# Two spectral layers and a scan on one core: row transforms moved into the items, the projections and the scan's output

## The chip, the cores and the metric

The kernel runs on one core of one Trainium2 chip. The metric is the time of one execution in device microseconds (us). The kernel before took 3879.38 us (median of 3 runs, 3878.82 to 3880.02).

## The reference

An image of 48 x 48 positions and 768 channels, in 32-bit floats, goes through four layers: a vision transformer block, a spectral layer, a scan and a second spectral layer with other weights. The change touches the last three. Cut to what matters (a pair of numbers in `w[0], w[1]` is real and imaginary part):

```python
def spectral(x):                          # layers 1 and 3
    xs = rfft2(x, axes=(1, 2)).reshape(B, H, W // 2 + 1, 8, 96)
    xr, xi = real(xs), imag(xs)
    o1r = relu(xr @ w1[0] - xi @ w1[1] + b1[0])   # per block of 96 channels
    o1i = relu(xi @ w1[0] + xr @ w1[1] + b1[1])
    o2r = o1r @ w2[0] - o1i @ w2[1] + b2[0]
    o2i = o1i @ w2[0] + o1r @ w2[1] + b2[1]
    out = softshrink(o2r, 0.01) + 1j * softshrink(o2i, 0.01)
    return irfft2(out, s=(H, W), axes=(1, 2)) + x

def scan(x):                              # layer 2
    B_, C_, X, alpha, theta, gamma = projections(x)   # x @ W + b, silu or sigmoid
    for i in range(12):
        inj = rope(B_, theta * (i + 1)) * X
        h = alpha * conv3x3_depthwise(h) + (1 - gamma) * alpha * prev + gamma * inj
        prev = inj
    return silu((rope(C_, theta * 12) * h).reshape(48, 48, 256) @ W_out + b_out)
```

## The kernel before

**Names.** TensorE is PE, VectorE DVE, ScalarE ACT, GpSimd POOL and SyncE SP; SP only issues DMAs. The 768 channels are cut into two halves of 384 (`TB`), each into three column tiles of 128 (`ct`) and four blocks of 96 (`b`). The 48 image rows are cut into 6 groups `g` of 8 rows. `yu[half]` is a scratch array in DRAM that holds the half-spectrum along w of one half of the channels. A matmul of 32-bit floats is two instructions in the profile.

**The instructions' order.** Each engine carries out its instructions in an order that is fixed when the kernel is built. The program text sets it roughly; the builder moves instructions that are ready ahead of others, and loads above all. Waits come from the tiles: a tile of a pool with `bufs` buffers is free again when the last reader of its predecessor is done.

**First spectral layer, `afno_first` (L1529).** The transform along w (`spectrum_rows` L1361, here within `afno_follow`) is largely carried out in the layer before. `spectrum_mix` then works on 40 items: half (1, then 0), five groups of frequencies `kc`, four blocks `b`. An item is pipelined over 5 steps by a table of stages: the transform along h (`f_x`, L1420), first matrix (`f_o`, L1434 to L1436), second matrix and softshrink (`f_z`, L1455 to L1461) and the transform back along h (`f_u`, L1470). There are 44 steps; the last four, in which no new item begins, are the drain. After four blocks the tile `us` is stored to `yu` on SP (L1477). When all items are done, the transform back along w follows for half 1, then half 0: for each g the tile `gt` is loaded on SP (`load_spectrum` L1491, three buffers), and for each of 3 column tiles four matmuls with `gt` as the stationary operand and `iw` as the moving one (L1557) fill a PSUM bank, which ACT or DVE in turn copies into `x2T`, the scan's input with the channels on the partitions: 6 column tiles of 48 rows of 64 columns.

**Scan, `scan_phase` (L1000).** It opens with the DVE's memset of four pairs of PSUM banks `pss` (L1043) and POOL's memsets of the state (`H`, `al`, `c1`, `s0`, `s1`: L1045 to L1047). Then come the projections: for each of 24 pairs of image rows `pr`, two groups of 6 matmuls (357 and 256 columns, L1082) into one pair of banks, which DVE empties, adding the bias (L1084). After each 3 pairs a chain of DVE and ACT instructions makes sines, sigmoids and products of them (8 blocks `q`). The scan's 12 steps follow. Its output (L1230 to L1246): for each two pairs of rows (`p2`, 12 of them) four transposes, a copy on ACT to `hT`, then for each pair and half two matmuls (L1243), the bias on DVE (L1245) and silu on ACT (L1246) into `x3`.

**Second spectral layer, `afno_second` (L1564).** After the scan's output: the transform along w for 12 groups (half 0, then 1, L1361; stored on SP), `spectrum_mix` with half 0 first, and the transform back for half 0, then half 1: load `gt` (four buffers), four matmuls (L1588), the addition into `x3` on DVE (L1590), and the store to the output on ACT's queue (L1594), or, for the last group of each half, four stores on ACT's and SP's queues in turn (L1592).

Of the kernel before, what the change touches and what calls it, by code (L numbers as in the profile page):

```python
# [11 lines left out]
F32 = mybir.dt.float32  # L12
BF16 = mybir.dt.bfloat16
AF = mybir.ActivationFunctionType
ALU = mybir.AluOpType
AX = mybir.AxisListType
PSUM = bass.MemoryType.PSUM
DRAM = bass.MemoryType.DRAM

P = 128  # L20
# [979 lines left out]
def scan_phase(tc, ident, w, w_close, wts, xT, xT_close, c_d, cr_d, out_open):  # L1000
# [21 lines left out]
    with tc.tile_pool(name="sc_s", bufs=1, side="left") as sp:  # L1022
# [9 lines left out]
        with (  # L1032
# [9 lines left out]
            for ps in pss:  # L1042
                V.memset(ps, 0.0)  # L1043
# [4 lines left out]
            with (  # L1048
# [10 lines left out]
                def temp(shape, tag, q, bufs=1):  # L1059
                    return tp.tile([P, *shape], F32, tag=tag, name=f"{tag}_{q}", bufs=bufs)[:K]  # L1060
# [10 lines left out]

                for q in range(NQ):
# [3 lines left out]
                    for t in range(R4):  # L1076
                        tok = (q * R4 + t) * P
                        ps = pss[(q * R4 + t) % 4]
                        parts = ((za, 0, NA), (g, NA, NCR))
                        for i, (z, c0, n) in enumerate(parts):  # L1080
                            for cc in range(NC):
                                nc.tensor.matmul(ps[:K, i, :n], lhsT=xT[:, cc, tok : tok + K], rhs=w[:, cc, c0 : c0 + n], start=cc == 0, stop=cc == NC - 1)  # L1082
                        for i, (z, c0, n) in enumerate(parts):
                            V.tensor_tensor(z[:, :, t], ps[:K, i, :n], bias[:K, c0 : c0 + n], ALU.add)  # L1084
# [30 lines left out]
                    gc = temp([NM, R4], "gc", q)  # L1115
# [27 lines left out]
            w_close()  # L1143
            xT_close()
# [80 lines left out]
        with (  # L1225
            tc.tile_pool(name="so_t", bufs=3, side="left") as tp,
            tc.tile_pool(name="so_q", bufs=2, space=PSUM) as pt,
            tc.tile_pool(name="so_p", bufs=6, space=PSUM) as pm,
        ):
            for p2 in range(NPR // 2):  # L1230
                ps = pt.tile([P, 512], F32, tag="t", name=f"ht_{p2}")
                for t in range(2):
                    for j in range(2):
                        nc.tensor.transpose(ps[:, (2 * t + j) * P : (2 * t + j) * P + K], hg[:K, 2 * p2 + t, j * P : (j + 1) * P], ident[:K, :K])
                hT = tp.tile([P, 4, 2, G], F32, tag="hT", name=f"hT_{p2}")
                nc.scalar.copy(hT, ps.rearrange("p (i s w) -> p i s w", i=4, s=2)[:, :, :, :G])
                for t in range(2):
                    pr = 2 * p2 + t
                    for half in range(2):
                        cols = slice(half * TB, (half + 1) * TB)  # L1240
                        ps = pm.tile([P, 512], F32, tag="m", name=f"so_{pr}_{half}")
                        for j in range(2):
                            nc.tensor.matmul(ps[:BS, :TB], lhsT=hT[:, 2 * t + j].rearrange("p s w -> p (s w)"), rhs=wo[:, j, cols], start=j == 0, stop=j == 1)  # L1243
                        t_ = tp.tile([BS, TB], F32, tag="t", name=f"st_{pr}_{half}")
                        V.tensor_tensor(t_, ps[:BS, :TB], bo[:, cols], ALU.add)  # L1245
                        nc.scalar.activation(x3[:, pr, cols], t_, AF.Silu)  # L1246
    return x3
# [15 lines left out]
def block_kernel(ctx: ExitStack, tc: tile.TileContext, a: dict):  # L1263
# [69 lines left out]
    x2T, x2T_close = opened("x2T", [P, NC, G * HD], "right")  # L1333
    wsc, wsc_close = opened("wsc", [P, NC, a["W_scan"].shape[1]], "right")
    afno_first(tc, a, yu, x2T, follow_in, lambda: nc.sync.dma_start(wsc, a["W_scan"].rearrange("(c p) n -> p c n", p=P)))
# [11 lines left out]
    x3 = scan_phase(tc, ident, wsc, wsc_close, wts, x2T, x2T_close, c_d, cr_d, out_open)  # L1347
    afno_second(tc, a, x3, yu)
# [17 lines left out]
def spectrum_mix(tc, name, a, layer, yu, psum, keep, side, halves, beside):  # L1366
# [8 lines left out]
    w1, b1, w2, b2 = (a[f"{layer}_{k}"] for k in ("w1", "b1", "w2", "b2"))  # L1375
    HB = NB // 2
    with (
        tc.tile_pool(name=f"{name}_c", bufs=1, side=side) as cp,
        tc.tile_pool(name=f"{name}_y", bufs=3, side=side) as yp,
        tc.tile_pool(name=f"{name}_s", bufs=2, side=side) as sp,  # L1380
    ):
        fh = cp.tile([BS, BS], F32, tag="fh", name=f"{name}_fh")
        nc.sync.dma_start(fh, a["fh"])
        w1t = cp.tile([BS, NB, 2, BS], F32, tag="w1", name=f"{name}_w1")
        w1s, w1d = (cp.tile([BS, NB, BS], F32, tag=n, name=f"{name}_{n}") for n in ("w1s", "w1d"))
        w2t = cp.tile([BS + 1, NB, 2, BS], F32, tag="w2", name=f"{name}_w2")
        b1t = cp.tile([BS, 2, NB], F32, tag="b1", name=f"{name}_b1")
        ih = cp.tile([BS, BS], F32, tag="ih", name=f"{name}_ih")
        ys = {}

        def load(half, kc):
            yt = yp.tile([BS, KC, TB], F32, tag="yt", name=f"{name}_yt_{half}_{kc}")
            nc.sync.dma_start(yt, yu[half][4 * KC * kc : 4 * KC * (kc + 1)].rearrange("(k q) p c -> (q p) k c", q=4))
            us = sp.tile([BS, KC, TB], F32, tag="us", name=f"{name}_us_{half}_{kc}")
            ys[half, kc] = yt, us

        nc.sync.dma_start(w1t, w1)
        nc.sync.dma_start(b1t, b1)
        nc.sync.dma_start(w2t[:BS], w2)
        nc.sync.dma_start(w2t[BS : BS + 1], b2)  # L1400
        nc.sync.dma_start(ih, a["ih"])
        nc.gpsimd.tensor_tensor(w1s, w1t[:, :, 0, :], w1t[:, :, 1, :], ALU.add)
        nc.gpsimd.tensor_tensor(w1d, w1t[:, :, 1, :], w1t[:, :, 0, :], ALU.subtract)
# [9 lines left out]
        def s_fft_h(i):  # L1413
            half, kc, b = items[i]
            if b == 0:
                load(half, kc)
# [112 lines left out]
def afno_first(tc, a, yu, x2T, follow_in, load_next):  # L1529

    nc = tc.nc
    ev = Evac(nc)
    x2v = x2T.rearrange("p c (h w) -> p c h w", w=HD)
    nc.gpsimd.memset(x2v[:, :, :, G:], 0.0)
    with (
        tc.tile_pool(name="f1_g", bufs=1, side="right") as gp,  # L1540
        tc.tile_pool(name="f1_p", bufs=8, space=PSUM) as pm,
    ):

        def psum(tag):
            return pm.tile([P, 512], F32, tag="m", name=f"f1_{tag}")

        iw = gp.tile([4 * KW, BS], F32, tag="iw", name="f1_iw")
        follow = follow_in(gp, 1)
        spectrum_mix(tc, "f1", a, "L1", yu, psum, True, "left", (1, 0), lambda step: follow(psum) if step in (1, 4) else load_next() if step == 8 else None)
        nc.sync.dma_start(iw, a["iw"])  # L1550
        for half in (1, 0):
            for g in range(NTB):
                gt = load_spectrum(nc, gp, yu, half, g, "f1", 3)
                for ct in range(NC // 2):
                    ps = psum(f"w_{half}_{g}_{ct}")
                    for i in range(4):
                        nc.tensor.matmul(ps[:, i * BS : (i + 1) * BS], lhsT=gt[: 4 * KW, i, ct * P : (ct + 1) * P], rhs=iw, start=True, stop=True)  # L1557
                    ev(x2v[:, half * NC // 2 + ct, 8 * g : 8 * g + 8, :G], ps[:, :TB].rearrange("p (h w) -> p h w", w=G))


def afno_second(tc, a, x3, yu):
# [4 lines left out]
    with (  # L1566
        tc.tile_pool(name="f3_g", bufs=1, side="left") as gp,
        tc.tile_pool(name="f3_p", bufs=8, space=PSUM) as pm,
    ):
# [3 lines left out]
        nc.sync.dma_start(iw, a["iw"])  # L1573

# [3 lines left out]
        for half in range(2):  # L1578
            for g in range(NTB):
                spectrum_rows(nc, fw, x3[:, 4 * g : 4 * g + 4, half * TB : (half + 1) * TB], yu, half, g, psum, gp, ev, "f3")  # L1580
        spectrum_mix(tc, "f3", a, "L3", yu, psum, False, "left", (0, 1), lambda step: None)
        for half in range(2):
            cols = slice(half * TB, (half + 1) * TB)
            for g in range(NTB):
                gt = load_spectrum(nc, gp, yu, half, g, "f3", 4)
                for i in range(4):
                    ps = psum(f"w_{half}_{g}_{i}")
                    nc.tensor.matmul(ps[:BS, :TB], lhsT=iw, rhs=gt[: 4 * KW, i, :], start=True, stop=True)  # L1588
                    dst = x3[:, 4 * g + i, cols]
                    nc.vector.tensor_tensor(dst, ps[:BS, :TB], dst, ALU.add)  # L1590
                    if g == NTB - 1:
                        (nc.scalar, nc.sync)[i % 2].dma_start(out[:, 4 * g + i, cols], dst)  # L1592
                if g < NTB - 1:
                    nc.scalar.dma_start(out[:, 4 * g : 4 * g + 4, cols], x3[:, 4 * g : 4 * g + 4, cols])  # L1594
# [112 lines left out]
```

## Time and profile before

| | before |
|---|---|
| median of 3 runs | 3879.38 us |
| the profiled execution | 3878.45 us |
| its span in the profile | 3876.6 us |
| PE busy | 3761.5 us, 97% of the span |
| DVE, ACT, POOL busy | 2059.0, 1141.9, 658.4 us |
| DMA | 460.43 MB, 119 GB/s |
| first layer's items end, transform back along w begins | 3049.3 us |
| projections | 3112.5 to 3264.1 us |
| first matmul of the scan's steps | 3275.6 us |
| scan's output and transform along w | 3528.5 to 3630.8 us |
| second layer's items | 3634.5 to 3830.8 us |
| last DVE addition | 3873.4 us |

The span is the time between the first and the last instruction of the profiled execution; 1.85 us lie around it. All points in time in the text are counted from the span's start. A line of groups shows engine and operation, output and inputs with their shapes, the number of instructions, then busy time, mean ns of one, and the idle time ahead of them with what ended it. A line of the timeline shows start, duration, instruction, and in brackets the wait ahead of it. The clock is the share of TensorE's full clock that was granted.

### The profile page before, as it was taken

The numbers are of one execution on the slowest core, as the hardware profiler recorded it, in microseconds if no ns is written. First come the engines' busy times: TensorE is split into PE (matmuls) and PEld (weight loads), VectorE is DVE, ScalarE is ACT, GpSimd is POOL, SyncE is SP. The second block draws the span as 40 slices with busy tenths as digits, with TensorE's granted clock in tenths as the row PEclk, the third lists the DMA queues.
The fourth block names the chain that finished last, engine by engine and source line by source line (L and its number), as shares of the span: only waits on it lengthen the run. The fifth ranks groups of instructions, "written<-read, shape, count | busy, mean of one in ns | idle before, by whom it ended". The sixth has DMA issues, their size and how long they took to land. (4 is left out here: it accounts for less than half of the span.)

```text
span 3876.6 us, 54460 instructions
## 1 busy us (share of the span) xinstructions
PE 3761.5 (97%) x22018; PEld 2285.7 (59%) x22018; DVE 2059.0 (53%) x3185; ACT 1141.9 (29%) x1907; POOL 658.4 (17%) x496
## 2 busy tenths in 40 slices
PE   8999989999999999998999999999999998999998
PEld 4666544444444444455555555555568866996685
DVE  6655456666666666555425333232335367995355
ACT  1322244444444444421310120021023246223341
POOL 3101011111111111024000000000023301981131
PEclk9999989999999999999999999999999799999999
DMA  7656563424232322134334434433454302110444
GB/s 257 210 187 197 173 183 112 127 92 133 84 110 83 105 87 76 36 95 161 123 105 155 150 107 124 147 122 108 132 139 110 96 24 93 40 32 22 146 108 159
DMA packets 266810, 460.43 MB, mean 119 GB/s; under 512 B 32989, under 2 KB 219349, under 8 KB 260055
## 3 DMA queue, kind: packets, MB, share of 16 engines
q1 hardware_dynamic: 256919, 436.23, 36.3%
q10 hardware_dynamic: 9632, 20.65, 1.4%
q8 instruction: 175, 2.87, 0.3%
q14 instruction: 84, 0.69, 0.1%
HBM read 318.49 MB, written 138.31 MB: 118 GB/s over the span
## 5 line engine op out<-in xcount | busy, mean ns | idle before, releaser
L576 DVE TENSOR_TENSOR acc<-acc,p 128x768 f32<-128x768 f32 x576 | 582.8, 1012 | 354.9 <-ACT p L568 316.5
L568 ACT ACTIVATE p<-s 128x768 f32<-128x768 f32 x648 | 478.5, 812 | 692.7 <-PE s L566 580.5
L929 PE MATMUL p<-w,h 128*128 128x384 f32 x1512 | 492.7, 486 | 0.0
L558 PE MATMUL s<-qt,kv 64*128 64x384 f32 x2592 | 478.5, 501 | 9.1 <-ACT p L568 7.4
L587 PE MATMUL av<-p,kv 128*64 128x384 f32 x2592 | 464.5, 493 | 0.0
L929 PEld LDWEIGHTS p<-w,h 128*128 128x128 f32 x1512 | 286.1, 190 | 196.9
L558 PEld LDWEIGHTS s<-qt,kv 64*128 64x128 f32 x2592 | 233.1, 187 | 249.9 <-ACT p L568 116.0
L587 PEld LDWEIGHTS av<-p,kv 128*64 128x64 f32 x2592 | 170.0, 136 | 225.2 <-issue 215.8
L866 PE MATMUL p<-x2nT,w 128*128 128x384 f32 x864 | 294.0, 490 | 3.1 <-issue 3.1
L294 PE MATMUL qk<-xnT,wqk 128*128 128x384 f32 x756 | 252.5, 491 | 5.2 <-DMA wqk<-wqk_d 5.2
L1172 PE MATMUL c<-H,bands 128*48 128x96 f32 x5632 | 242.8, 247 | 12.1 <-issue 11.5
L566 PE MATMUL s<-bt,oneh 120*128 120x384 bf16 x1296 | 248.3, 328 | 0.0
L1172 PEld LDWEIGHTS c<-H,bands 128*48 128x48 f32 x5632 | 234.2, 123 | 20.9 <-issue 11.9
L866 PEld LDWEIGHTS p<-x2nT,w 128*128 128x128 f32 x864 | 165.4, 192 | 119.1 <-issue 6.0
L866 PE MATMUL p<-xT,w 128*128 128x384 f32 x648 | 220.8, 486 | 0.0
L566 PEld LDWEIGHTS <-oneh 120*128 120x128 bf16 x1296 | 109.1, 98 | 174.3 <-issue 115.1
L294 PEld LDWEIGHTS qk<-xnT,wqk 128*128 128x128 f32 x756 | 144.6, 193 | 99.9 <-issue 8.5
L905 POOL TENSOR_TENSOR rr<-rr,ml_b 128x1152 f32<-128x1152 f32 x12 | 33.5, 2788 | 954.4 <-DMA rr<-xr_d 660.8
L861 ACT ACTIVATE h<-h,ml_b 128x384 f32<-128x384 f32 x144 | 88.3, 614 | 346.6 <-DVE h L881 174.3
L1180 POOL TENSOR_TENSOR t<-s,c 128x768 f32<-128x768 f32 x80 | 144.8, 1836 | 214.3 <-DVE s L1142 203.8
L866 PEld LDWEIGHTS p<-xT,w 128*128 128x128 f32 x648 | 123.1, 190 | 85.9
L1082 PE MATMUL c<-wsc,x2T 128*112 128x357 f32 (+1 forms) x576 | 151.6, 426 | 2.0 <-DVE c L1043 2.0
(314 smaller groups left out, 4778.7 us busy)
## 6 DMA issues: line engine op xcount, KB each, us to landing
w<-w1s_d SPq DMA_DIRECT2D x36, 768.0 KB
w<-w2s_d SPq DMA_DIRECT2D x36, 768.0 KB
bt<-rh_d SPq DMA_DIRECT2D x144, 162.0 KB
w<-w1s_d SPq DMA_DIRECT2D x36, 576.0 KB
w<-in_mlp_w_dram SPq DMA_DIRECT2D x27, 768.0 KB
wqk<-wqk_d SPq DMA_DIRECT2D x12, 1344.0 KB
yu<-f_ys SPq DMA_DIRECT2D x24, 672.0 KB
f_gt<-yu SPq DMA_DIRECT2D x24, 672.0 KB
```

The lines of the kernel that those rows point to most:

```text
L294: nc.tensor.matmul(p[:, :TB], lhsT=w[:, n, c, :], rhs=ops[sb][n][:, c, :], start=c == 0, stop=c == NC2 - 1)
L558: nc.tensor.matmul(ps[:, s, :QB], lhsT=keys[pr % 2][rows, kt * P : (kt + 1) * P], rhs=qbs[qc % 2][0][rows], start=True, stop=False)
L566: nc.tensor.matmul(ps[:, s, :QB], lhsT=oneh[:NBR, b % 3, :], rhs=qbs[qc % 2][1][:NBR, s, b // 3, j, :], start=False, stop=True)
L568: nc.scalar.activation(p, ps[:, :, :QB], AF.Exp)
L576: nc.vector.tensor_tensor(probs[c], probs[c], p, ALU.add)
L587: nc.tensor.matmul(avs[c][rows, :QB], lhsT=vals[pr % 2][:, kt, rows], rhs=p[:, s, :], start=kt == 0, stop=kt == NT - 1)
L861: nc.scalar.activation(h, h, AF.Gelu, bias=b1c[:, k : k + 1])
L866: nc.tensor.matmul(p[:, :TB], lhsT=w[n][:, c, :], rhs=rhs[n][:, c, :], start=c == 0, stop=c == NC2 - 1)
L929: nc.tensor.matmul(ps[t][:, :TB], lhsT=hs[left, f][:, t * P : (t + 1) * P], rhs=wt[:, f % KW2, :], start=f == 0, stop=f == NF2 - 1)
L1082: nc.tensor.matmul(ps[:K, i, :n], lhsT=xT[:, cc, tok : tok + K], rhs=w[:, cc, c0 : c0 + n], start=cc == 0, stop=cc == NC - 1)
L1172: nc.tensor.matmul(ps[r0 : r0 + G, k // 4, cols], lhsT=bands[:, n - GC, i, :] if gr else bands0[:, n, i, :], rhs=H[:, n, :, d : d + NPR], ...
L1180: GP.tensor_tensor(t, sc[:, ch], c1[:, m0 : m0 + GC].unsqueeze(2).to_broadcast([P, GC, RR, NPR]), ALU.mult)
```

## The change

It has three parts.

1. *First spectral layer and projections.* `x2T` is replaced by `xh`, which holds half 1 only, and two small tiles `homes` of 8 image rows each for half 0. Half 1's transform back for g = 0 to 3 is issued within the drain (steps 40 to 43), with `gt` loaded at steps 28, 30, 32 and 34 (four buffers instead of three), and for g = 4 and 5 after it. Half 0's transform back of one group (`rows_back`) is called within the projections: ahead of the first pair of rows, and then at every fourth (`pr % 4 == 2`, for the group after the current one). Its column tiles use the two banks of the fourth PSUM pair in turn; the projections keep three pairs. The sum over the 6 column tiles runs in reverse, half 1 first. The temporary `gc` takes the buffer of `th`.
2. *Scan's output.* It becomes a generator with two passes: half 0 for all 12 `p2`, then half 1, with the 12 tiles `hT` kept. After every second `p2` the caller issues `spectrum_rows` of the group before, in the same pass, with the scan's PSUM banks. The second layer's weights (`spectrum_open`, split off from `spectrum_mix`) are loaded at the scan's end; the first three tiles of half 0's spectrum are loaded during the second pass.
3. *Second spectral layer.* Half 0's transform back is issued within the items, at steps 32, 35, 38, 40, 41 and 42, with its first four loads at steps 27, 29, 31 and 33. Only half 1's stays behind the items, with four loads ahead. The last group of half 0 is stored in one piece.

```diff
-            for ps in pss:
+            for ps in pss[:3]:
                 V.memset(ps, 0.0)
...
+                turn_of = itertools.cycle(range(2))
+                banks = lambda tag: pss[3][:, next(turn_of), :]
+                xs = [rows_back(0, banks)]
...
-                        tok = (q * R4 + t) * P
-                        ps = pss[(q * R4 + t) % 4]
+                        pr = q * R4 + t
+                        if pr % 4 == 2 and pr + 4 < NPR:
+                            xs.append(rows_back(pr // 4 + 1, banks))
+                        x_of = lambda cc: (xs[pr // 4], cc, pr % 4 * P) if cc < NC // 2 else (xh, cc - NC // 2, pr * P)
+                        ps = pss[pr % 3]
...
-                            for cc in range(NC):
-                                nc.tensor.matmul(ps[:K, i, :n], lhsT=xT[:, cc, tok : tok + K], rhs=w[:, cc, c0 : c0 + n], start=cc == 0, stop=cc == NC - 1)
+                            for cc in reversed(range(NC)):
+                                v, c, tok = x_of(cc)
+                                nc.tensor.matmul(ps[:K, i, :n], lhsT=v[:, c, tok : tok + K], rhs=w[:, cc, c0 : c0 + n], start=cc == NC - 1, stop=cc == 0)
...
-            for p2 in range(NPR // 2):
+            yield x3, psum
+            hTs = []
+            for half in range(2):
+                cols = slice(half * TB, (half + 1) * TB)
+                for p2 in range(NPR // 2):
+                    if half == 0:
...
+                        hT = tp.tile([P, 4, 2, G], F32, tag=f"hT{p2}", name=f"hT_{p2}", bufs=1)
...
+                    yield
...
+        def back(half, g, dst, psum):
+            gt = gts.pop((half, g))
+            for ct in range(HC):
+                ps = psum(f"w_{half}_{g}_{ct}")
+                for i in range(4):
+                    nc.tensor.matmul(ps[:, i * BS : (i + 1) * BS], lhsT=gt[: 4 * KW, i, ct * P : (ct + 1) * P], rhs=iw, start=True, stop=True)
+                ev(in_rows(dst)[:, ct, :, :G], ps[:, :TB].rearrange("p (h w) -> p h w", w=G))
...
+        def first_back(g):
+            back(1, g, xh[:, :, 8 * g * HD : 8 * (g + 1) * HD], psum)
+            if g + 4 < NTB:
+                load(1, g + 4)
...
+            elif last - 12 <= step < last - 4 and step % 2 == 0:
+                load(1, (step - last + 12) // 2)
+            elif step >= last:
+                first_back(step - last)
...
+        for g in range(4, NTB):
+            first_back(g)
+            load(0, g - 4)
...
+    def rows_back(g, banks):
+        if g + 2 < NTB:
+            load(0, g + 2)
+        back(0, g, homes[g % 2], banks)
+        return homes[g % 2]
...
+        def rows_in(n, psum):
+            half, g = ready[n]
+            spectrum_rows(nc, fw, x3[:, 4 * g : 4 * g + 4, half * TB : (half + 1) * TB], yu, half, g, psum, gp, ev, "f3")
+            if NTB <= n < NTB + 3:
+                opened[1](0, n - NTB)
...
+        for n, _ in enumerate(scan):
+            if n and n % 2 == 0:
+                rows_in(n // 2 - 1, scan_psum)
+            if n == 4 * NTB - 1:
+                rows_in(2 * NTB - 1, scan_psum)
...
-        for half in range(2):
-            for g in range(NTB):
-                spectrum_rows(nc, fw, x3[:, 4 * g : 4 * g + 4, half * TB : (half + 1) * TB], yu, half, g, psum, gp, ev, "f3")
-        spectrum_mix(tc, "f3", a, "L3", yu, psum, False, "left", (0, 1), lambda step: None)
...
+        loads = {items - 13 + 2 * g: g for g in range(4)}
+        backs = {items - 8: 0, items - 5: 1, items - 2: 2, items: 3, items + 1: 4, items + 2: 5}
+
+        def beside(step):
+            if step in loads:
+                load(0, loads[step])
+            if step in backs:
+                g = backs[step]
+                back(0, g)
+                if g + 4 < NTB:
+                    load(0, g + 4)
+
+        spectrum_mix(tc, "f3", opened, yu, psum, False, "left", (0, 1), beside)
+        for g in range(4):
+            load(1, g)
+        for g in range(NTB):
+            back(1, g)
+            if g + 4 < NTB:
+                load(1, g + 4)
```

## The prediction

> **What bounds the kernel now.** I read first the page, for the engine that bounds and for its clock.
>
> ```profile
> PE 3761.5 (97%) x22018; PEld 2285.7 (59%) x22018; DVE 2059.0 (53%) x3185; ACT 1141.9 (29%) x1907; POOL 658.4 (17%) x496
> ...
> PEclk9999989999999999999999999999999799999999
> ```
>
> PE is busy for 97% of the span, so waits can give back only 115 us in all. The clock is the second lever: the 32nd slice (96.9 us each, so 3004 to 3101) runs at 0.7. That is where the first spectral layer ends. So I asked for a table of stages around the three edits (us; then PE, PEld, DVE, ACT, POOL; clock; DMA share; GB/s).
>
> ```profile
> core 0: us, PE busy (x) PEld busy (x) DVE busy (x) ACT busy (x) POOL busy (x), PEclk, DMA share, GB/s
> 3049.00:3111.00 62.00, 61.46 (x290) 61.01 (x288) 10.63 (x19) 9.90 (x19) 23.19 (x6) 0.51 0.42 125
> 3112.00:3264.00 152.00, 151.53 (x576) 102.63 (x576) 111.06 (x282) 86.71 (x147) 0.00 (x0) 0.98 0.08 24
> 3264.00:3276.00 12.00, 0.49 (x7) 0.47 (x8) 9.96 (x32) 10.16 (x19) 0.00 (x0) 0.68 0.86 315
> 3528.00:3598.00 70.00, 68.71 (x235) 35.64 (x233) 28.02 (x52) 30.39 (x60) 0.00 (x0) 0.98 0.01 2
> 3598.00:3631.00 33.00, 31.85 (x97) 16.66 (x96) 11.76 (x23) 10.05 (x24) 3.58 (x2) 1.00 0.76 237
> 3631.00:3650.00 19.00, 12.66 (x57) 10.81 (x58) 2.79 (x7) 5.04 (x12) 3.64 (x5) 0.56 0.66 208
> 3650.00:3830.00 180.00, 177.02 (x1464) 148.56 (x1464) 89.92 (x175) 72.44 (x171) 54.93 (x75) 1.00 0.31 82
> 3830.00:3877.00 47.00, 36.74 (x98) 16.98 (x98) 27.24 (x49) 0.00 (x0) 0.00 (x0) 0.88 0.84 284
> ```
>
> Three rows are weak. The back-transforms of the first spectral layer (first row) fill PE at half clock. The start of the second layer's items (3631 to 3650) is a third idle and at half clock. The tail (last row) has the DMA engines at 84%. The projections (second row) are full of PE work at full clock, while DVE and ACT are busy for 111 and 87 of 152 us.
>
> Then the groups of the first row, and PE's timeline just before it:
>
> ```profile
> L1557 PE MATMUL f_w<-f_iw,f_gt 100*128 100x96 f32 x288 | 61.2, 419 | 0.0
> L1557 PEld LDWEIGHTS f_w<-f_iw,f_gt 100*128 100x128 f32 x288 | 61.1, 331 | 0.5 <-issue 0.5
> ```
>
> ```profile
> 3044.18 1.05 PE L1470 MATMUL f_u<-f_Z,f_ih 96*96 96x480 f32 x2 [1.43 <-DVE f_Z L1461]
> ...
> 3048.45 1.02 PE L1470 MATMUL f_u<-f_Z,f_ih 96*96 96x480 f32 x2 [1.53 <-DVE f_Z L1461]
> 3049.30 5.05 PE L1557 MATMUL f_w<-f_iw,f_gt 100*128 100x96 f32 x25
> ```
>
> 288 instructions in 61.2 us are 212 ns apart. The stage begins after a drain in which PE waited 1.43 and 1.53 us for Z, and the clock falls just there.
>
> [...]the mean clock is 0.50 from 3049.9 to 3118.0 and 1.00 after it. [...]61 us of unbroken back-transforms did not bring the clock back, full projections did. [...]The 212 ns here are twice that, at half clock; 107 ns is my estimate for full clock, which this trace does not show for this form. [...]Here that store took 4.5 us (issued 3050.18, landed 3054.7).[...]
>
> **Part 1, first layer's backs.** Removed: the 62 us stage and the cold start of the projections (3112.5 to 3118.0 at half clock: 2.75 us). The 36 column tiles of 8 instructions remain: per half 144 instructions x 107 ns = 15.4 us, 2.57 per group of rows.
>
> Half 1, in the drain. The last o matmul ends at 3039.6. Then, in the build's order on PE: back 0 (2.57), u (0.85), z (1.7), back 1, u, z, back 2, u: 3053.2, where before the last u ended at 3049.3. The waits of 1.43 and 1.53 for Z are covered by backs, so the clock should stay up (other windows with 67 to 73% PE busy did; one with 55%, 3046.5 to 3049.9, did not). Backs 3 to 5 take 7.7 more: 3060.9. The last store is issued at 3054.1, lands at 3058.6 (4.5), and half 0's first load lands at 3062.5 (3.7, as a load with free queues took). Evacuation and the DVE memset of three PSUM pairs end at about 3062.8. So the projections start at 3062.8 instead of 3112.5. SP's queue: half 0's loads stand behind the last store and behind nothing else that is late; bias and W_scan are loaded long before. POOL's memsets (23.2 us, after the store has landed) end near 3082, about when the first block of three row pairs asks for them; before they had 30 us to spare, so this cover is thin, but the parts asked for first (al, c1, s) come ahead of the last.
>
> Half 0, in the projections: 148.8 us (151.6 less 2.75) + 15.4 + 1.7[...] + 3 for stalls of two rotating banks (six groups, half a microsecond each). Sum 168.9: end 3231.7 against 3264.1. Three PSUM pairs instead of four cost nothing: an evacuation takes 1.13 us and trails PE by at most 2, a pair of rows takes 6.2. The added 9 evacuations on DVE (0.56 each) and 9 on ACT (0.48) lie beside PE. The gap of 11.5 us ahead of the scan is the last block's chain and stays. **Gain 32 us.** If the backs stay cold in the drain, the start slides to 3070 and the gain is 24; with no stalls and no cold window it is 37.
>
> **Part 2, scan's output in two passes.** The matmuls and evacuations are the same (102 us for both rows, 3528 to 3631); only their order changes. Removed is the start of the items:
>
> ```profile
> 3634.51 1.89 PE L1420 MATMUL f_x<-f_fh,f_yt 96*96 96x96 f32 x10 [3.71 <-issue]
> ...
> 3647.65 0.53 PE L1455 MATMUL f_z<-f_w,f_o 97*96 97x96 f32 x2
> ```
>
> PE waited 3.7 us for the stored spectrum, went cold, and reached the first z at 3647.65. Afterwards half 0's spectrum has landed long before. At full clock this start takes 2 x 0.85 for x, 1.2 for o and 1.4 of waits each, from 3631: the first z at about 3639, 8.6 earlier, and 1.3 for z that ran cold. Gain 10[...]: **9**. Bounds: 13 with no wait; 3 if a row of x3 is late for the transform (ACT's silu comes before it) or the weights now loaded at the scan's end are late.
>
> **Part 3, second layer's backs.** Half 0's 48 instructions (2.65 us per group warm, from 0.33 us spacing) move into the items: 15.9 us, of which the three in the drain fill waits of about 3. The last u ends 12.4 later. The tail now starts with the same latency and half the bytes:
>
> ```profile
> 3830.91 14.61 PE f_w L1588 x40
> ...
> 3860.16 7.40 DMA f_gt<-yu
> ...
> 3867.69 5.13 PE f_w L1588 x8
> ...
> 3872.84 0.56 DVE x L1590
> ```
>
> Last u at 3843.1, store issued 3844.5, landed 3849.8 (5.3, beside out stores), first load 3854; PE is idle 10 us and cold for the first group (5.1), the last load is asked for at 3862, takes 7.4, and 2.6 of matmuls and the add end at 3872.5, against 3873.4. What was hidden behind half 0's backs, the round trip of the last store, is now bare. **Gain about 0**, from +7 (slower) to -5. The six out stores of half 0 stay on ACT's queue, now among the items' copies; I cost their issue at nothing, since ACT is busy for 72 of 180 us there. Without that cover each would hold up one f_X copy and the next o matmul by about the time of one copy, 3 us in all.
>
> **Sum.** -32.4 - 9 + 0 = -41.4 against the profiled execution: 3878.45 (its span 3876.6 and 1.85 around it), which is 0.9 below the median of 3879.38. 3878.45 - 41.4 = 3837.
>
> **Rivals.** A, cold backs: the drain does not hold the clock. For it: 61 us of this very form ran cold. Against it: they began cold. Part 1 gives 24: about 3846, chance 0.14. B, streams that give nothing: transform rows wait for silu, or the tail grows by 7. Part 2 or part 3 falls out: 3844 to 3853, say 3850, chance 0.14. C, slower: two banks for the column tiles. Their evacuations stand in order behind the block's chain on DVE and ACT, where single instructions take 0.5 to 1.3 us; if a tile waits for five of them, 3 us x 18 tiles = 54 on PE: 3891. It decides from 41.4 / 18 = 2.3 us per tile. Against it:
>
> ```profile
> PE c L1082 <- DVE c L1043: 2.0, 1, 2.0
> ```
>
> PE's only wait in the projections was the memset ahead of them; evacuations there were never late, on four pairs. Chance 0.07. D: half 0's loads sit behind something on SP and the projections start as late as before; only part 2 stays, less what the mixed-in backs cost: near 3875, chance 0.03.
>
> **How the numbers follow.** My forecast has 0.62. The range 3822 to 3860 takes the best bounds of parts 1 and 2 (-37, -13, tail -5 gives 3823) and A and B together. About 0.2% is what a measurement of this kernel can tell from no change. Faster: 0.62 + 0.14 + 0.14 = 0.90; the same 0.03; slower 0.07.
>
> **What would show it.** Right: after the last u of the first layer the backs are 107 ns apart and the clock row reads 0.9 or more; the projections start about 50 us earlier and last about 169; waits of PE for evacuations in them sum to under 5; the second layer's first x follows the last transform without a gap; about 33 us lie between the last u and the end. Wrong: backs at 212 ns, PE waiting for ACT or DVE in the projections by more than 20 us, or a tail of over 40 us.

## The result and the profile after

The changed kernel took 3841.59 us (median of 4 runs, 3836.77 to 3842.16) against 3879.1 us for the kernel before on the same chip (4 runs): a ratio of 0.990, 95% interval 0.9883 to 0.9918. That is 37.5 us less, where 41.4 were forecast. The profiled execution took 3841.45 us, its span is 3839.7.

The page's first lines, then the stages that answer to those shown of before (same columns):

```profile
PE 3727.7 (97%) x22018; PEld 2255.4 (59%) x22018; DVE 2057.3 (54%) x3184; ACT 1142.8 (30%) x1908; POOL 656.5 (17%) x498
...
PEclk9999989999999999999999999999999999999999
```

```profile
core 0: us, PE busy (x) PEld busy (x) DVE busy (x) ACT busy (x) POOL busy (x), PEclk, DMA share, GB/s
3039.80:3063.80 24.00, 22.05 (x192) 20.46 (x190) 11.44 (x20) 5.08 (x11) 5.58 (x2) 1.00 0.48 133
3063.80:3232.00 168.20, 167.63 (x720) 117.85 (x720) 113.52 (x288) 91.75 (x157) 18.45 (x6) 0.99 0.15 42
3232.00:3244.50 12.50, 0.18 (x1) 0.00 (x0) 10.40 (x33) 11.50 (x20) 0.00 (x0) 0.61 0.93 325
3496.60:3598.20 101.60, 100.58 (x328) 52.93 (x328) 39.97 (x72) 40.84 (x85) 3.60 (x2) 0.98 0.38 110
3598.20:3611.50 13.30, 9.00 (x56) 7.67 (x56) 4.18 (x11) 4.08 (x9) 3.08 (x5) 0.74 0.16 53
3611.50:3804.00 192.50, 192.50 (x1516) 156.31 (x1514) 102.35 (x199) 72.61 (x171) 55.60 (x76) 1.00 0.36 99
3804.00:3815.80 11.80, 0.01 (x1) 0.00 (x0) 0.65 (x1) 0.00 (x0) 0.00 (x0) 0.68 0.78 216
3815.80:3839.70 23.90, 18.75 (x48) 8.97 (x48) 13.29 (x24) 0.00 (x0) 0.00 (x0) 0.86 0.89 270
```

PE executes as many instructions as before (22018), but is busy for 33.8 us less, and the 7 in the clock row is gone: the same work ran faster. PE's share of the span is 97% as before, so a reader of the first line alone would have seen nothing. The stage of the transform back at half clock (62 us at 0.51) is gone: half 1's part lies in the 24 us of drain at 1.00, half 0's within the projections. Of the places that the change touches, two are still weak: the start of the second layer's items (13.3 us at 0.74) and the tail.

The end of the first layer, from PE's timeline:

```profile
3045.00 2.84 PE L1588 MATMUL f_w<-f_iw,f_gt 100*128 100x96 f32 x24
3047.68 0.97 PE L1503 MATMUL f_u<-f_Z,f_ih 96*96 96x480 f32 x2
...
3053.68 8.18 PE L1588 MATMUL f_w<-f_iw,f_gt 100*128 100x96 f32 x72
3063.86 3.55 PE L1094 MATMUL c<-wsc,xh 128*112 128x357 f32 x6 [2.01 <-DVE c L1047]
```

The last but one u of the drain, shown here, no longer waits for Z; 24 instructions take 2.7 us, 112 ns each. The projections begin at 3063.86 (forecast 3062.8). The wait of 2.01 us ahead of them, the memset of their banks, costs them the clock once: it is 0.55 from 3063.86 to 3067.40, where six instructions take 3.55 us, against 1.96 later on.

### The profile page after: what moved, and what is told of

It reads as the page before. It is cut to its first block, busy times and chain, and to the rows that moved or that the text cites. A ratio compares the mean times of both kernels' runs of the same rounds, so it can differ in the third digit from the quotient of the medians.

```text
span 3839.7 us, 54414 instructions
## 1 busy us (share of the span) xinstructions
PE 3727.7 (97%) x22018; PEld 2255.4 (59%) x22018; DVE 2057.3 (54%) x3184; ACT 1142.8 (30%) x1908; POOL 656.5 (17%) x498
## 4 chain that ended last, share of the span: by engine, by line
PE 93%; DVE 2%; DMA 2%; issue 1%; ACT 1%; POOL 1%; SPq 0%; DVEq 0%; ACTq 0%; POOLq 0%
PE p L867 13%; PE p L930 12%; PE s L559 12%; PE av L588 12%; PE c L1183 6%; PE s L567 6%; PE qk L295 6%; PE c L1094 4%; PE v L164 3%; PE pj L164 2%; PE f_z L1489 2%; PE f_z L1488 2%; PE f_x L1453 2%; PE so L1263 2%; PE f_u L1503 2%; PE rh L415 1%
## 5 line engine op out<-in xcount | busy, mean ns | idle before, releaser
L597 DVE RECIPROCAL rec<-rs 128x384 f32<-128x384 f32 x36 | 92.1, 2558 | 100.6 <-PE rs L595 100.6
```

## The experiments

All were timed against the kernel before on the chip that they shared with it. "Gain" is the difference to its median; the changed kernel's own is 37.5 us. The chips were not always the same, and the intervals of most gains are 5 to 7 us wide to each side. Much of that comes from ahead of the change: in the profiles of these kernels the last o matmul of the first spectral layer ends anywhere from 3034.0 to 3041.5 us. Differences of a few us are therefore read from the length of a stage in the timelines as well (us, one profiled execution each):

| stage | before | changed | its part taken out | edited further |
|---|---|---|---|---|
| end of the last o of the first layer to the scan's first matmul (part 1) | 235.8 | 204.5 | 235.8 | |
| first matmul of the scan's output to the first z of the second layer (part 2) | 119.1 | 113.7 | 120.2 | 106.5 (two groups of the transform moved) |
| that z to the end (part 3) | 229.0 | 229.3 | 229.9 | 223.9 (three groups left for the tail) |

In the kernels that leave part 1 as it is, the first of these stages takes 204.4 to 204.6 us.

**Each part taken out.** The first three kernels undo one part each; without part 1, `afno_first` and the projections are those of before.

```diff
-    xh, xh_close = opened("xh", [P, NC // 2, G * HD], "right")
+    xh, xh_close = opened("xh", [P, NC, G * HD], "right")
...
-                xs = [rows_back(0, banks)]
...
-                        ps = pss[pr % 3]
+                        ps = pss[(q * R4 + t) % 4]
```

> The changed kernel without its part 1: the first spectral layer's transform back and the projections stand as before; parts 2 and 3 stay. If the parts add up and the profile of the changed kernel is read rightly (part 1 is worth 31 us there), about 3873 us. If part 1's gain was made at the expense of something that parts 2 and 3 pay for, or they are worth more than the 6 us read, under 3868. If they are worth nothing, 3879.

3871.09 against 3877.34 us, ratio 0.9984 (0.9978 to 0.9991): a gain of 6.3. Part 1 is worth 31.3 of the 37.5, the same as in the table (235.8 less 204.5).

```diff
+        for _ in scan:
+            pass
...
+        for n in range(2 * NTB):
+            rows_in(n, psum)
+        opened = spectrum_open(tc, stack, "f3", a, "L3", yu, "left")
```

> The changed kernel without its part 2: the scan's output takes both halves together, and the transform along w and the second layer's weights come after it, as before; parts 1 and 3 stay. By the reading of the profile (6 us) about 3847 us. By the 9 us of the prediction 3850. If only the wait of 3.7 us counted, 3845. The clock should be at half for some 17 us around the first items again.

3845.88 against 3877.34, ratio 0.9919 (0.9905 to 0.9932): a gain of 31.5, so part 2 is worth 6.0 (6.5 by its stage). The wait for the stored spectrum is back in PE's timeline, and half clock with it, for about 13 us (17 expected):

```profile
3605.29 1.89 PE L1448 MATMUL f_x<-f_fh,f_yt 96*96 96x96 f32 x10 [3.81 <-issue]
```

```diff
+        spectrum_mix(tc, "f3", opened, yu, psum, False, "left", (0, 1), lambda step: None)
+        for half in range(2):
+            for g in range(NTB):
+                load(half, g)
+                back(half, g)
```

> The changed kernel without its part 3: both halves' transforms back come after the second layer's items, as before; parts 1 and 2 stay. Predicted and read: part 3 is worth nothing, so 3841 us, 3837 to 3845. Rival: halving the tail's bytes was worth something, 3846 or more. Rival: the 16 us of matmuls put into the items cost more than the tail gives back, 3835 or less.

3839.4 against 3877.34, ratio 0.9902 (0.9887 to 0.9917): a gain of 37.9. Part 3 is worth nothing that can be measured (-0.4; +0.6 by its stage). The chain of waits shows the old tail, in which it puts the last load behind 14 us of output stores:

```profile
3806.55 14.15 DMA out_dram<-x
...
3820.76 7.47 DMA f_gt<-yu
...
3828.37 5.42 PE f_w L1682 x8
```

The three parts add up: 31.3 + 6.0 - 0.4 = 36.9.

**Is part 1 the clock, or the placement?** First, all of half 1's groups behind the drain:

```diff
-            elif step >= last:
-                first_back(step - last)
...
-        for g in range(4, NTB):
+        for g in range(NTB):
             first_back(g)
```

> The changed kernel with half 1's six groups all behind the drain, none in it. If the clock is the cause of part 1's gain, [...]half 1's 144 instructions run 212 ns apart instead of 107 (15 us more), the projections begin at half clock, and with the two waits for Z uncovered (3 us) less the 2 us that PE now waits ahead of the projections the time is about 3858 us. If the gain is only the placement of half 0's part within the projections, 3 us more than the changed kernel: 3845.

3859.31 against 3877.34, ratio 0.9956 (0.9942 to 0.9969): 19.5 us of the gain are lost (18.7 by the stage), near what the clock theory had (16), not 3. The group of half 1's transform back and the timeline in front of it:

```profile
L1588 PE MATMUL f_w<-f_iw,f_gt 100*128 100x96 f32 x144 | 30.0, 413 | 0.0
```

```profile
3047.03 1.02 PE L1503 MATMUL f_u<-f_Z,f_ih 96*96 96x480 f32 x2 [1.52 <-DVE f_Z L1494]
3047.89 30.05 PE L1588 MATMUL f_w<-f_iw,f_gt 100*128 100x96 f32 x144
```

144 instructions in 30.0 us: 208 ns. The waits for Z are bare again, and the clock fell behind them (0.84 from 3046.5 to 3049.9, 0.50 from there to 3053.3).

Then the opposite, the clock without any change of place. The kernel before gets idle work in its drain:

```diff
+            if keep and len(items) <= step < len(items) + 3:
+                ps = psum(f"fill_{step}")
+                for i in range(4):
+                    nc.tensor.matmul(ps[:BS, :TB], lhsT=fh, rhs=ys[halves[-1], NKC - 1][0][:, i, :], start=True, stop=True)
```

> The kernel before with twelve matmuls added in the drain of the first spectral layer, four ahead of each of the three last u; their result is not used, and nothing else is moved: both halves' transforms back stay behind the items, the projections behind them. The added work is 7.9 us, 3 of it in waits for Z. Theory, the clock is the cause: [...]the 288 instructions of the transform back run 107 ns apart at full clock (30.8 us instead of 61.2), the projections no longer begin cold: about 26 us faster than before, 3851. Rival, the pattern of the transform back itself cannot hold the clock[...], and what helped in the changed kernel was mixing it with other matmuls: 3870 to 3882.

3877.03 against 3876.75, ratio 0.9999 (0.999 to 1.0007). The clock theory as I had put it missed by 26 us, and the rival's number came out. PE's timeline says why:

```profile
3052.94 8.18 PE L1561 MATMUL f_w<-f_iw,f_gt 100*128 100x96 f32 x72
3062.53 45.60 PE L1561 MATMUL f_w<-f_iw,f_gt 100*128 100x96 f32 x216 [1.41 <-DMA f_gt<-yu]
```

The filled drain kept the clock: three groups ran at 114 ns an instruction. The clock is the third column from the right (1.00, then 0.51):

```profile
3052.90:3061.10 8.20, 8.20 (x73) 8.01 (x71) 2.88 (x5) 1.91 (x4) 2.61 (x1) 1.00 0.78 215
3062.50:3108.00 45.50, 45.47 (x216) 45.38 (x216) 7.24 (x13) 7.26 (x14) 19.17 (x6) 0.51 0.43 123
```

PE was now faster than the loads, of which three buffers allow three at a time. It waited 1.41 us for the fourth, and the 216 instructions after that wait are 211 ns apart. So the rival (the pattern cannot hold the clock) and a third possibility (it holds it until a wait, and then cannot win it back) were both open. One buffer more for `gt` tells them apart:

```diff
-                gt = load_spectrum(nc, gp, yu, half, g, "f1", 3)
+                gt = load_spectrum(nc, gp, yu, half, g, "f1", 4)
```

> The kernel before with the twelve added matmuls in the drain (their result not used) and four buffers for gt instead of three. With three, the transform back ran at full clock for three groups, then waited 1.41 us for its fourth load and stayed at half clock for the other nine. With four the fourth load is there before it begins and each later one is asked for 10 us ahead. Clock theory: full clock throughout, 288 instructions 107 to 113 ns apart, 3850 to 3854 us. If a load is late once more, half clock from that point: 3860 to 3875. If the pattern cannot hold the clock by itself, half clock within the first groups without any wait before it: 3872 or more.

3851.82 against 3877.57, ratio 0.993 (0.9916 to 0.9943): a gain of 25.8, with nothing moved.

```profile
3052.36 32.30 PE L1561 MATMUL f_w<-f_iw,f_gt 100*128 100x96 f32 x288
3086.66 43.53 PE L1082 MATMUL c<-wsc,x2T 128*112 128x357 f32 x160 [2.01 <-DVE c L1043]
```

All 288 instructions run in one piece at 112 ns: 32.3 us instead of 61.2. Twelve matmuls whose result nobody uses and one more buffer are worth 26 us. The buffer alone, without the twelve, was not run; but in the kernel before PE was idle for 0.0 us ahead of these 288 instructions, so it never waited for a load there. The twelve make the drain 3.9 us longer (13.6 us from the last o to the last u, against 9.7). With these given back, the gain would be about 30 by this estimate, close to part 1's 31. That the backs lie among the items and the projections is therefore worth little in itself; it is what keeps the clock without idle work. For half 0's groups in one block ahead of the projections, in the changed kernel, there is no measurement: the six tiles do not fit beside the projections' buffers.

**The slower rival: banks.** One bank for the column tiles instead of two:

```diff
-                turn_of = itertools.cycle(range(2))
+                turn_of = itertools.chain([1], itertools.repeat(0))
```

> The changed kernel with one PSUM bank instead of two in turn for the column tiles within the projections (all but the first). It prices the slower rival: how long an evacuation stands in the queues of DVE and ACT. With two banks PE waited 0.5 us in all. If a tile waits only for its predecessor's evacuation (some 1 us from the last matmul), and other matmuls stand between some of them, 3 to 10 us more than the changed kernel: 3845 to 3851. If an evacuation stands behind the block's chain for 3 us, as the rival had it, 17 x 3 = 51 more: 3890.

3838.73 against 3877.57, ratio 0.99 (0.9885 to 0.9915): a gain of 38.8, the same as the changed kernel. PE's waits from 3060 to 3235:

```profile
PE c L1588 <- ACT x L58: 0.5, 1, 0.5
```

Even one bank makes PE wait only 0.5 us, and the stage takes 204.4 us, as with two. The timeline shows the reason: the build puts the tiles apart, in the first two groups with two or more instructions of the projections between them, so each evacuation has time. The first group:

```profile
3061.27 1.03 PE L1588 MATMUL c<-f_iw,f_gt 100*128 100x96 f32 x8
3062.14 0.78 PE L1094 MATMUL c<-wsc,xh 128*112 128x357 f32 x2
3062.91 1.13 PE L1588 MATMUL c<-f_iw,f_gt 100*128 100x96 f32 x8
```

My expectation (3 to 10 us more) was too high as well.

**Where part 2 fell short.** In the changed kernel PE waited at the first two items and ran at half clock there (0.50 from 3604.2 to 3607.6). The last two groups of the transform along w, not needed before the 21st item, can fill these waits:

```diff
-            if n and n % 2 == 0:
+            if n and n % 2 == 0 and n // 2 - 1 < 2 * NTB - 2:
                 rows_in(n // 2 - 1, scan_psum)
...
         def beside(step):
+            if step < 2:
+                rows_in(2 * NTB - 2 + step, psum)
```

> The changed kernel with the last two groups of the transform along w (half 1, not needed before the 21st item) taken out of the scan's output and put behind the first f_x of the first two items, where PE waited 1.45 and 1.70 us for f_Xs and lost its clock. Theory: the waits and the half clock of the start cost 3.1 and 3.4 us, so about 6 us faster than the changed kernel, 3835. Rival: the wait of 1.15 us ahead of the first item grows by as much, or the clock falls there all the same: 3839 to 3842.

3831.2 against 3876.75, ratio 0.9879 (0.9864 to 0.9894): a gain of 45.6, 8 more than the changed kernel, where 6 were expected. The intervals of the two gains overlap; the stage is 7.2 us shorter. In PE's timeline the waits for f_Xs at the first two items and the half clock are gone (one of 0.72 us ahead of the first item is left):

```profile
3591.38 1.09 PE L1453 MATMUL f_x<-f_fh,f_yt 96*96 96x96 f32 x10 [0.72 <-DVE st L1265]
3592.30 2.76 PE L1389 MATMUL f_f<-x,f_fw 96*112 96x384 f32 x8
3594.90 0.57 PE L1467 MATMUL f_o<-f_Xs,f_w 96*96 96x240 f32 x2
```

**Where part 3's gain went.** Three of half 0's groups left for the wait in the tail:

```diff
-        backs = {items - 8: 0, items - 5: 1, items - 2: 2, items: 3, items + 1: 4, items + 2: 5}
+        backs = {items: 0, items + 1: 1, items + 2: 2}
...
+        for g in range(3, NTB):
+            back(0, g)
         for g in range(4):
             load(1, g)
```

> The changed kernel with three of half 0's groups in the drain of the second layer's items, none among full items, and three behind the drain, where PE waited 11.8 us for the last store and its load. If that wait is latency, these 7.7 us of matmuls fit into it: about 3834 us. If the tail is bound by the DMA engines (busy for 78 and 89% of its two parts), the three stores of the output that now fall into it take that back: 3839 to 3842.

3834.82 against 3876.75, ratio 0.9891 (0.9876 to 0.9906): a gain of 41.9, 4.4 more than the changed kernel (5.4 by the stage), close to the first expectation (3834). The chain of waits in the tail:

```profile
3795.65 6.36 DMA yu<-f_us
...
3802.20 7.78 DMA f_gt<-yu
3809.98 0.14 issue
3810.11 17.45 PE f_w L1682 x48
```

7.7 us of matmuls fit into the wait, but the last store now takes 6.36 us and the load after it 7.78, with the output stores of these groups beside them; in the changed kernel they took 5.42 and 5.51. That is 3.2 us given back. That these stores are the reason is likely, but was not tested apart.

**Both, and one more.** These two edits together:

> The changed kernel with both edits: the last two groups of the transform along w in the first two items, and three of half 0's groups left for the tail. They lie 190 us apart, so the gains should add: 8 and 4 us, 3828 us (3825 to 3831). If they share something[...], 3831 or more.

3829.32 against 3877.57, ratio 0.9872 (0.9857 to 0.9887): a gain of 48.3, the fastest kernel of this study, 10.8 more than the changed kernel where the two edits alone had 8 and 4.4 (the difference is within the intervals; by the stages 9.9). Adding a third edit, half 1's groups 4 and 5 behind the change of PSUM pools:

```diff
-        for g in range(4, NTB):
-            first_back(g)
-            load(0, g - 4)
...
     def rows_back(g, banks):
+        if g == 0:
+            rest(banks)
```

> As rows_and_tail, and half 1's last two groups (4 and 5) carried out in the projections' two spare banks, behind the change of the PSUM pools, so that the memset of the projections' banks on DVE runs beside them instead of making PE wait 2.0 us and lose its clock for 3.3 us. If so, about 1 us of the wait and the 1.7 us of half clock go: 3825. If PE waits as long one step earlier, at the change of pools, as rows_and_tail or up to 2 us more.

3832.23 against 3877.57, ratio 0.9878 (0.9863 to 0.9893): no better, and the first stage is 2.1 us longer (206.7). PE's waits from 3052 to 3235 show what took the place of the 2.0 us:

```profile
PE c L1588 <- ACT x L58: 1.1, 2, 0.6
PE c L1588 <- DVE x L60: 0.7, 1, 0.7
PE c L1588 <- issue: 0.7, 1, 0.7
PE c L1588 <- ACT xh L58: 0.6, 1, 0.6
PE c L1094 <- ACT x L58: 0.6, 1, 0.6
```

3.7 us in six waits. In four of them (the first, second and fourth line) a column tile waits for an evacuation: here column tiles follow one another with nothing between them, and two banks are too few. That is the rival's mechanism, at 0.6 us a tile instead of 3.

## Why the prediction was right, and where it was off

The forecast was 3837 us; 3841.6 was measured. Point by point, by the profile:

*Part 1, forecast -32.4, measured -31.0 at the scan's first matmul (3244.54 against 3275.56), -31.3 by taking it out.* The chronology of the drain held to about 1 us: the last u ends at 3053.7 (forecast 3053.2), backs 3 to 5 at 3061.9 (3060.9), the projections begin at 3063.86 (3062.8). They last 168.3 us (168.9), but two terms of that sum were off and happened to cancel: the 3 us for stalls of two banks were too many (0.5), and the 18 tiles cost about 2 us more than the 15.4 forecast. An instruction of theirs takes 112 ns in a row, not the 107 of the estimate from 212 ns at half clock, which is 0.7 us of it; the rest is what is left of the sum, and was not traced further. The 1.7 us in the sum were my estimate for half clock at the start; there it cost 1.6 (3.55 us for six instructions instead of 1.96). The gap ahead of the scan grew from 11.5 to 12.35 us. The reason given, the clock, is what the runs show: the kernel before, with a filled drain and four loads, has most of the gain with nothing moved. My rival A (the backs stay cold in the drain) was wrong here, but it is one wait of 1.4 us away, as that kernel with three loads shows. Its price was too low: where half 1's backs did run cold, behind the drain, the projections began at 3083.05, not at the 3070 that I had for it. The prediction did not say that the loads in time are part of what keeps the clock. In the kernel before with the filled drain they are; the changed kernel with three `gt` buffers was not run.

*Part 2, forecast -9, measured -6.* This is the term that was mis-sized, "At full clock this start takes 2 x 0.85 for x, 1.2 for o and 1.4 of waits each"; the 0.9 between its gain of 10 and its 9 was my estimate for half clock. From the last transform to the first z I had 8.0 us (the terms as written give 6.9; the third x ahead of the first z, 0.85, was not named in them); it took 12.2 (3598.2 to 3610.4):

```profile
3599.36 1.06 PE L1453 MATMUL f_x<-f_fh,f_yt 96*96 96x96 f32 x10 [1.15 <-issue]
3601.87 0.65 PE L1467 MATMUL f_o<-f_Xs,f_w 96*96 96x240 f32 x2 [1.45 <-POOL f_Xs L1457]
...
3606.36 1.11 PE L1467 MATMUL f_o<-f_Xs,f_w 96*96 96x240 f32 x2 [1.70 <-POOL f_Xs L1457]
3607.26 1.01 PE L1468 MATMUL f_o<-f_X,f_w1d 96*96 96x240 f32 x2
```

The clock there, again the third column from the right:

```profile
3600.80:3604.20 3.40, 2.33 (x15) 2.09 (x16) 1.31 (x5) 0.94 (x3) 0.69 (x1) 0.90 0.40 137
3604.20:3607.60 3.40, 1.70 (x6) 1.17 (x6) 0.00 (x0) 1.14 (x4) 1.47 (x2) 0.50 0.00 0
3607.60:3611.00 3.40, 3.40 (x21) 2.99 (x20) 0.71 (x2) 1.48 (x4) 0.42 (x1) 0.60 0.00 0
```

1.15 us of it is a wait ahead of the first x. The profile doesn't name its cause; 0.1 us before it ends, DVE has emptied the last bank of the scan's PSUM pool, after a memset for the items (0.66 us) that it carried out first. Another 0.35 is what the two waits for f_Xs are longer than forecast, and the rest is mainly the half clock, which, worked out from these means, lasts from about 3603.5 to 3610.3: the o matmuls take 1.01 us there, and 0.57 at full clock. Taking the 3.7 us away left waits of 1.15 and 1.45 us within 4 us, and after these two the clock was lost; the third, of 1.70 us, lies within the half clock already. I had them in the sum as waits and did not ask what they do to the clock, the very question that decided part 1. The transform's last groups fill them, and that gains 8 us.

*Part 3, forecast 0, measured +0.4 by taking it out.* The items became 10.3 us longer from the first z to the last u (193.6, before 183.3; forecast 11.1), the tail 10.0 shorter (35.7, before 45.7; forecast 13). The tail's first pieces came out as they were written, each a little longer. The last load, on which the prediction had PE wait once more, did not hold it up: all 48 matmuls run in one piece.

```profile
3804.77 5.42 DMA yu<-f_us
...
3810.26 5.51 DMA f_gt<-yu
...
3815.82 18.76 PE f_w L1682 x48
```

PE idles 11.8 us (forecast 10). The gain that one might expect of such a change, half the bytes behind the items, is given back by what half 0's backs had hidden before: the store's landing and the first load.

*The slower rival* was wrong in its price: the point from which it decides was 2.3 us per tile, and PE waited 0.5 us in 18 tiles. The order on DVE and ACT, in which it had the evacuations stand, is the same in the traces of both kernels up to 2840 us (2075 and 1193 instructions that work on tiles); that an evacuation stands there for 3 us was my estimate, and no trace shows it.

Single waits were enough to cost the clock: after 1.41 us (for the fourth load, with three buffers) it was 0.51 for the 45.5 us up to 3108, and after 2.01 us (ahead of the projections of the changed kernel) 0.55 from 3063.86 to 3067.40.

## What to carry to other kernels

When PE is busy for 97% of the span, look at the clock by stage before looking for waits: the same instructions took 61 or 32 us, and two waits of 1.4 and 1.5 us ahead of them decided which. A short wait is not priced by its length alone but by what stands behind it; fill it with work that has to be done anyway, and check that PE, once it is faster, does not run into its loads. Moving work out of a tail gains only what it does not uncover: ask first what that work was hiding.

## What the runs showed of the hardware that was not expected

The same row of matmuls (100 x 96 moving, 128 columns stationary) held full clock (112 ns an instruction) over 32.3 us where it began with it and had no wait, and ran at half clock in its stretches of 45.6 and 61.2 us, where the clock fell at their start (0.50 from 3063.80 on, after a begin at 3062.53, and from 3050.0 on, after 3049.30): in these runs it did not win the clock back. The projections (357 and 256 columns moving) won it back within 6 us (in the kernel before 0.50 from 3112.5 to 3118.0 and 1.00 from there to 3260, in the changed one from 3063.9 to about 3067.6). In the tail two transfers of 0.7 MB, each waiting for the one before, took 10.9 us in sum in the changed kernel, and 14.1 and 14.5 in `three_left_for_tail` and `rows_and_tail`, which put three more output stores (1.7 MB) off until then.
